# Graph network of four layers: the weighted sum of one layer on VectorE instead of TensorE, and later places for the work behind the sums

## The chip, the cores and the metric

The kernel runs on one core of a Trainium2 chip. The metric is the time of one launch on the device, in microseconds, from the median of several runs; lower is better. The five engines are named as the profile names them: PE is TensorE (its weight loads are listed apart as PEld), DVE is VectorE, ACT is ScalarE, POOL is GpSimd and SP is SyncE.

## The reference, cut to what matters

Four graph layers are applied to `x`, 4096 rows of 256 float32 values. `adj` is a 4096 x 4096 matrix of 0 and 1; it is sparse (each row has itself and a few neighbours, some 9 in the mean), so an attention over all 4096 columns comes down to a weighted sum over each row's neighbours.

```python
h = relu(layernorm(x)); x = x + L0(h, adj)   # four heads, elu of the result
h = relu(layernorm(x)); x = x + L1(h, adj)   # one head
h = relu(layernorm(x)); x = x + L2(h, adj)   # four heads, with a bias
h = relu(layernorm(x)); x = x + L3(h, adj)   # dot products, four heads

# L0, and L2 in the same form
Wh = (h @ W).reshape(n, heads, d)
e = leaky_relu(s_i[:, None, :] + s_j[None, :, :], 0.2)   # s_i, s_j: Wh times two vectors
alpha = softmax(where(adj == 0, -inf, e), axis=1)
out = einsum('ijh,jhd->ihd', alpha, Wh)                  # L0 returns elu(out)

# L1: the neighbours' own rows are summed, not their products
h = node @ W
att = softmax(where(adj > 0, leaky_relu(s1[:, None] + s2[None, :], 0.01), NEG_INF), axis=1)
return h + att @ node

# L3
scores = q @ k.T / 8 + mask;  ctx = softmax(scores) @ v   # for each head, with biases
```

## The kernel before, in words

**The part that the change doesn't touch** takes the first 522 us or so. `scan` and `edges` turn the adjacency matrix into a list of up to 23 neighbours for every row. `first_table` writes the table of layer 0 (a row's product, with its two score terms). `early` takes the first six neighbours of each row in layer 0 already, and `sort` orders the rows by their number of neighbours into 32 blocks of 128 rows. Since the rows of a block have about the same number of neighbours, a block needs a fixed number of gathered rows, `CAPS`: 23 for the first, 3 for the last, 277 in the sum. In layer 0 only what exceeds six is left (93 in the sum, in 23 blocks).

**The layers** are four calls of `layer(l)`. Each walks over the 32 blocks in `ORDER`, a large block and a small one in turn. For one block the steps are:

- `fill(i)` has POOL issue the gathers of the blocks to come, up to `AHEAD` = 4 blocks ahead. Each gather (`fetch`, L529) is one indirect DMA that brings one neighbour for each of the 128 rows. They land in `s_ring`, a ring in SBUF with room for 69 gathered rows in layers 0 and 2, 64 in layer 1 and 36 in layer 3. A gather into a place waits until the last reader of that place is done. In layer 0 each block's own row is gathered as well; in layer 3 it is loaded by SP's queue.
- `scores` (L661 to L697) is DVE work on the block's gathered rows: the score terms are added, leaky_relu, the maximum, the subtraction; ACT then makes the exponentials, `s_p` (L697), in PSUM. In layer 1 it also checks the lists (`mutual`). In layer 3 the scores are products of 256 elements with the query: ACT first copies the query to PSUM (`s_q`), then DVE multiplies (L680) and reduces (L683), eight gathered rows at a time.
- `weigh` (L732 to L753): DVE sums the exponentials, inverts and scales them (L732 to L734); DVE scales the block's own row (L741), and PE adds it to a sum `s_acc` in PSUM by a product with the identity matrix (L745). Then, eight gathered rows at a time, DVE scales them in place (L749) and PE adds each to the sum by one more product with the identity (L753). PE's products with the identity are so 277 + 32 in each of the layers 1, 2 and 3, each of 256 float32 columns.
- `settle` adds the sum to `x`: L777 and L778 in layer 0 (with ACT's part of elu ahead of it), L780 in layers 1 and 2, L772 in layer 3. Then follows the layernorm of the next layer: `norms_of` has DVE's statistics (L382, L383), ACT's Ln and Exp (L386, L388), then four small DVE operations and ACT's relu (L507).
- `turned` has PE transpose the result (L515) and ACT copy it out of PSUM (L516); `times` has PE make the product with the next layer's weights (L522).
- `advance` has DVE take that product out of PSUM (L793 for layer 0's blocks, L800 for layer 1's, L807 and following for layer 2's) and write the next layer's table: POOL scatters it with an indirect DMA (L535) in layer 0, SP's queue sends it in layers 1 and 2 (L801, L808). In layer 3 POOL scatters the finished rows to the output with the same L535.

All layers hold the same loop. The order of the instructions on each engine is the order in which the program writes them (`manual_schedule`); the framework adds only the waits. So the order in the loop sets what each engine does first. With b the i-th block of the order, c the one before it and d the one before that, the loop writes: the gathers of the blocks ahead; the first part of c's settling; b's scores; d's norm, transposes and product; b's weighing; the rest of c's settling; and what comes after d's product. POOL's scatters stand behind that. A layer's first gathers need the whole table of the layer before.

PSUM has eight banks of 512 float32 columns. Before, two hold sums (`s_pacc`), three hold transposes and products (`s_pp`), one holds the query and two the exponentials (`s_pe`).

Of the kernel before, what the change touches and what calls it, by code (L numbers as in the profile page):

```python
# [9 lines left out]
F32 = mybir.dt.float32  # L10
# [4 lines left out]
ALU = mybir.AluOpType  # L15
AX = mybir.AxisListType
PSUM = bass.MemoryType.PSUM
DRAM = bass.MemoryType.DRAM

P = 128  # L20
D = 256
# [44 lines left out]
class Sparse:  # L66
# [246 lines left out]
    def first_table(self, pool, rows, r):  # L313
# [8 lines left out]
        for k in range(4):  # L322
# [5 lines left out]
            ps = self.times(self.turned(pool, h, f"t0_{t}"), self.we0, W, f"t0_{t}")  # L328
# [181 lines left out]
    def turned(self, pool, h, name):  # L510
# [3 lines left out]
        for c in range(KC):  # L514
            nc.tensor.transpose(pt[:, ts(c, P)], h[:, ts(c, P)], self.ident)  # L515
        nc.scalar.copy(ht, pt[:, : KC * P].rearrange("p (c r) -> p c r", c=KC))  # L516
        return ht
# [27 lines left out]
    def layers(self):  # L545
        tc, nc, nt = self.tc, self.nc, self.nt
        with ExitStack() as ctx:
            big = ctx.enter_context(tc.tile_pool(name="s_big", bufs=1))
            self.pool = ctx.enter_context(tc.tile_pool(name="s_main", bufs=2))
            self.pacc = ctx.enter_context(tc.tile_pool(name="s_pacc", bufs=2, space=PSUM))  # L550
            self.pp = ctx.enter_context(tc.tile_pool(name="s_pp", bufs=3, space=PSUM))
            self.pe = ctx.enter_context(tc.tile_pool(name="s_pe", bufs=3, space=PSUM))
# [19 lines left out]
    def layer(self, l):  # L572


# [30 lines left out]
        acc, behind, rows = {}, {}, {}  # L605

        def first(c):
            behind[c] = self.settle(l, c, acc.pop(c), made)
            next(behind[c])

        def second(d):
            if l < 3:
                ht = self.turned(self.pool, next(behind.pop(d)), f"{l + 1}_{d}")
                rows[d] = self.advance(l + 1, d, ht, made)
                next(rows[d])

        def third(d):
            if l < 3:
                next(rows.pop(d), None)
# [3 lines left out]

        for i in range(nt):
            fill(i)
            b, c, d = (ORDER[k] if k >= 0 else None for k in (i, i - 1, i - 2))
            if c is not None:
                first(c)
            g = ring[:, held[b][0] : held[b][1], :]
            p = self.scores(l, b, self.rows[b], g)  # L630
            if d is not None:
                second(d)
            acc[b] = self.weigh(l, b, vs.pop(b) if l == 3 else self.rows[b][:, 0:D], g, p)
            del held[b]
            if c is not None:
                next(behind[c])
            if d is not None:
                third(d)
        c, d = ORDER[-1], ORDER[-2]
        first(c)  # L640
        next(behind[c])
        second(d)
        second(c)
        third(d)
        third(c)

    def scores(self, l, b, mine, g):
# [25 lines left out]
        else:  # L673
            q = self.pe.tile([P, D], F32, name=f"s_q_{b}", tag="q", bufs=1)
# [21 lines left out]
        p = self.pe.tile([P, TOPK, H], F32, name=f"s_p_{l}_{b}", tag="p", bufs=2)  # L696
# [18 lines left out]
    def weigh(self, l, b, me, g, p):  # L715
# [22 lines left out]
        acc = self.pacc.tile([P, IB], F32, tag="acc", name=f"s_acc_{l}_{b}")  # L738
# [650 lines left out]
```

## Time and profile before

| what | value |
| --- | --- |
| time of the runs | 2269.25 us, median of 3 (2267.81 to 2284.88) |
| profiled execution | 2277.38 us |
| its span | 2275.6 us |
| mean granted TensorE clock | 0.75 |
| PE busy | 1175.5 us (52%), 3977 instructions |
| PEld busy | 795.2 us (35%), 3999 |
| DVE busy | 1270.9 us (56%), 3688 |
| ACT busy | 444.1 us (20%), 1320 |
| POOL busy | 1212.4 us (53%), 1354 |
| DMA packets | 128244, 313.24 MB, mean 138 GB/s |

Windows of the profile give the busy time of each engine in a stretch, then the mean granted clock of TensorE as a share of full speed, the DMA engines' busy share and the rate. Groups are listed as "line, engine, operation, out<-in by the program's names, count | busy us, mean ns of one | idle time of the engine just ahead of these instructions, and what ended it". "issue" means that nothing which the profile shows was waited for, and "remote" that the releaser is not among the instructions recorded on this core. Timeline lines have the start in us, the duration in us and the instruction; in brackets the idle time ahead of it on its engine and what ended it. The ends of matmuls are modelled, and a few of their records can be missing.

### The profile page before, as it was taken

The numbers are of one execution on the slowest core, as the hardware profiler recorded it, in microseconds if no ns is written. First come the engines' busy times: TensorE is split into PE (matmuls) and PEld (weight loads), VectorE is DVE, ScalarE is ACT, GpSimd is POOL, SyncE is SP. The second block draws the span as 40 slices with busy tenths as digits, with TensorE's granted clock in tenths as the row PEclk, the third lists the DMA queues.
The fourth block names the chain that finished last, engine by engine and source line by source line (L and its number), as shares of the span: only waits on it lengthen the run. The fifth ranks groups of instructions, "written<-read, shape, count | busy, mean of one in ns | idle before, by whom it ended". The sixth has DMA issues, their size and how long they took to land. (4 is left out here: it accounts for less than half of the span.)

```text
span 2275.6 us, 17106 instructions
## 1 busy us (share of the span) xinstructions
PE 1175.5 (52%) x3977; PEld 795.2 (35%) x3999; DVE 1270.9 (56%) x3688; ACT 444.1 (20%) x1320; POOL 1212.4 (53%) x1354
## 2 busy tenths in 40 slices
PE   4767677611466613454566333566668242445354
PEld 2434334301344402333445222344446131334233
DVE  7657787711466711444466313455569465667666
ACT  5754343000233300111111101112123100000000
POOL 1055666556455457566653375655660465666662
PEclk9887889855687855677788756778789665667777
DMA  8988885305233244333432243333331555666662
GB/s 271 297 288 308 300 259 178 88 13 108 75 99 102 76 88 114 93 104 106 111 104 73 57 110 86 102 100 93 109 107 45 145 171 156 182 181 184 179 180 66
DMA packets 128244, 313.24 MB, mean 138 GB/s; under 512 B 31844, under 2 KB 58983, under 8 KB 128136
## 3 DMA queue, kind: packets, MB, share of 16 engines
q0 software_dynamic: 69088, 207.53, 33.3%
q1 hardware_dynamic: 59048, 104.55, 13.6%
q8 instruction: 34, 0.56, 0.1%
q14 instruction: 74, 0.61, 0.1%
HBM read 276.91 MB, written 35.07 MB: 137 GB/s over the span
## 5 line engine op out<-in xcount | busy, mean ns | idle before, releaser
L529 POOL DMA_INDIRECT s_ring<-s_tab,s_near x924 | 878.0, 950 | 599.5 <-issue 239.8
L753 PE MATMUL s_acc<-s_ring,s_ident 128*128 128x256 f32 x1848 | 510.0, 434 | 80.8 <-issue 59.9
L753 PEld LDWEIGHTS s_acc<-s_ring,s_ident 128*128 128x128 f32 x1848 | 409.6, 224 | 179.1 <-issue 73.6
L745 PE MATMUL s_acc<-s_me,s_ident 128*128 128x256 f32 x256 | 107.7, 511 | 410.6 <-issue 135.3
L749 DVE TENSOR_TENSOR s_ring<-s_ring,s_p 128x256 f32<-128x256 f32 (+7 forms) x169 | 267.1, 1605 | 0.0
L529 POOL DMA_INDIRECT s_g<-s_tab,s_listrow x192 | 184.2, 960 | 113.0 <-issue 53.9
L301 DVE MAX8 s_cand<-s_pt 128x8 f32<-128x256 f32 x512 | 188.4, 419 | 81.6 <-remote 40.5
L745 PEld LDWEIGHTS s_acc<-s_me,s_ident 128*128 128x128 f32 x256 | 61.7, 253 | 436.0 <-issue 232.8
L522 PE MATMUL s_ps<-s_we_l,s_ht 128*128 128x264 f32 x256 | 107.5, 560 | 129.7 <-ACT s_ht L516 92.2
L780 DVE TENSOR_TENSOR s_rx<-s_rx,s_acc 128x256 f32<-128x256 f32 x64 | 26.7, 418 | 246.5 <-remote 240.0
L697 ACT ACTIVATE s_p<-s_e 128x32 f32<-128x32 f32 (+13 forms) x119 | 23.1, 194 | 715.1 <-DVE s_e L693 252.5
L293 PE MATMUL s_pt<-s_low,s_mark 128*128 128x512 fp8e4 x256 | 110.2, 430 | 95.9 <-DVE s_cand L301 45.1
L286 ACT ACTIVATE s_low<-s_raw 128x1024 fp8e4<-128x1024 int32 x128 | 134.5, 1051 | 55.0 <-DMA s_raw<-in_adj_dram 45.1
L522 PE MATMUL s_ps_kv<-s_wkv,s_ht 128*128 128x512 f32 x128 | 88.5, 829 | 94.2 <-issue 69.3
L370 PE MATMUL s_ae<-s_g,s_ident 128*128 128x256 f32 x384 | 111.0, 449 | 19.8 <-issue 11.2
L522 PEld LDWEIGHTS s_ps<-s_we_l,s_ht 128*128 128x128 f32 x256 | 59.9, 259 | 156.2 <-ACT s_ht L516 104.3
L299 PE MATMUL s_pt<-s_places,s_stands 128*128 128x512 bf16 x235 | 100.9, 430 | 0.0
L370 PEld LDWEIGHTS s_ae<-s_g,s_ident 128*128 128x128 f32 x384 | 84.5, 226 | 45.2 <-issue 17.0
L680 DVE TENSOR_TENSOR s_ring<-s_ring,s_q 128x2048 f32<-128x2048 f32 (+7 forms) x48 | 81.0, 1687 | 25.5 <-DMA s_ring<-s_tab,s_near 25.2
L515 PE MATMUL s_pht<-s_ident,s_h 128*128 128x128 f32 x128 | 28.9, 310 | 127.9 <-issue 88.1
L386 ACT ACTIVATE s_y<-s_mv,s_eps 128x1 f32<-128x1 f32 x96 | 28.3, 295 | 312.8 <-DVE s_mv L383 130.9
L772 DVE TENSOR_TENSOR s_out<-s_rx,s_acc 128x256 f32<-128x256 f32 x32 | 13.4, 418 | 133.4 <-remote 99.6
(180 smaller groups left out, 1591.3 us busy)
## 6 DMA issues: line engine op xcount, KB each, us to landing
s_raw<-in_adj_dram SPq DMA_DIRECT2D x128, 512.0 KB
s_ring<-s_tab,s_near POOLq DMA_INDIRECT x924
s_tab<-s_kv SPq DMA_DIRECT2D x32, 256.0 KB
s_own<-s_to SPq DMA_DIRECT2D x32, 134.0 KB
s_tab<-s_rows SPq DMA_DIRECT2D x8, 528.0 KB
s_tab<-s_rx SPq DMA_DIRECT2D x32, 132.0 KB
s_xl<-in_x_dram SPq DMA_DIRECT2D x8, 512.0 KB
s_own<-s_xl SPq DMA_DIRECT2D x8, 512.0 KB
```

What stands on the lines that cost most here:

```text
L286: nc.scalar.activation(lo[:, ts(h, quarter)], raw, AF.Copy, saturate=False, accum_out=sums[:, r, h : h + 1],)
L293: nc.tensor.matmul(pt, lhsT=self.mark, rhs=lo[:, ts(g, IB)], start=True, stop=False)
L299: nc.tensor.matmul(pt, lhsT=stands[:, g, :], rhs=places, start=False, stop=True)
L301: nc.vector.max(out=cand[:, g * (IB // CH) + k, :], in_=pt[:, ts(k, CH)])
L370: nc.tensor.matmul(acc[:, :D], lhsT=self.ident, rhs=g[:, k, 0:D], start=False, stop=(k == E - 1))
L515: nc.tensor.transpose(pt[:, ts(c, P)], h[:, ts(c, P)], self.ident)
L522: self.nc.tensor.matmul(ps[:, :width], lhsT=ht[:, c, :], rhs=w[:, c, :], start=(c == 0), stop=(c == KC - 1),)
L529: self.nc.gpsimd.indirect_dma_start(out=out, out_offset=None, in_=table[:, :], in_offset=bass.IndirectOffsetOnAxis(ap=idx, axis=0),)
L680: nc.vector.tensor_tensor(kq, kq, q.unsqueeze(1).to_broadcast([P, m, D]), ALU.mult)
L745: nc.tensor.matmul(acc[:, :D], lhsT=self.ident, rhs=mev, start=True, stop=(K == 0))
L749: nc.vector.tensor_tensor(v, v, p[:, k0 : k0 + m, :].unsqueeze(3).to_broadcast([P, m, H, D // H]), ALU.mult)
L753: nc.tensor.matmul(acc[:, :D], lhsT=self.ident, rhs=g[:, k0 + k, v0 : v0 + D], start=False, stop=(k0 + k == K - 1),)
```

## The change

1. In layer 1 the weighted sum is made by DVE alone: the own row is scaled into `s_acc` in PSUM, and then each gathered row is multiplied by its weight and added to `s_acc` with one `scalar_tensor_tensor`. DVE's scaling of gathered rows (L749) and own row (L741) and PE's products with the identity (L745, L753) are gone in this layer. Its weights `s_p` lie in SBUF instead of PSUM.
2. `turned` becomes a generator that stops between the transposes and the copy, so that other work can be written between the two.
3. The loop has a new order, with lags `S` and `N` that differ between layers. In layer 1 a block is settled at the end of its own round i (before: at the end of round i + 1); its norm and transposes are written at the start of round i + 1, ahead of the next block's scores (before: after the scores of round i + 2); the copy and the product follow those scores; and what comes after the product is written in round i + 2, right after the scores (before: at the end of round i + 2). In the layers 0, 2 and 3 a block's sum is settled two rounds later (before: one), after that round's scores (before: at the round's end); norm and transposes are three rounds later (before: two), ahead of the scores, with the copy and the product behind them; what comes after the product is four rounds later (before: two), right after the scores. POOL's scatters stand where that last step stands; in layer 3 a finished block is scattered right after the scores of the round that follows its settling (before: at the end of the round of its settling). The end of the layer is written out for the blocks that are left.
4. PSUM is shared out anew: four banks for sums, three for transposes and products as before, and one, `s_shares`, that holds the exponentials of two blocks in turn (in 96 columns each) and the query of layer 3 (in the last 256 columns).
5. The scaled own rows (`s_me`) have three buffers instead of two.

```diff
-        return ht
+        yield None
+        nc.scalar.copy(ht, pt[:, : KC * P].rearrange("p (c r) -> p c r", c=KC))
+        yield ht
...
-            self.pacc = ctx.enter_context(tc.tile_pool(name="s_pacc", bufs=2, space=PSUM))
+            self.pacc = ctx.enter_context(tc.tile_pool(name="s_pacc", bufs=4, space=PSUM))
+            shares = ctx.enter_context(tc.tile_pool(name="s_pe", bufs=1, space=PSUM))
             self.pp = ctx.enter_context(tc.tile_pool(name="s_pp", bufs=3, space=PSUM))
-            self.pe = ctx.enter_context(tc.tile_pool(name="s_pe", bufs=3, space=PSUM))
+            self.turns = 0
+            self.shares = shares.tile([P, IB], F32, name="s_shares")
...
-        def first(c):
-            behind[c] = self.settle(l, c, acc.pop(c), made)
-            next(behind[c])
-        def second(d):
-            if l < 3:
-                ht = self.turned(self.pool, next(behind.pop(d)), f"{l + 1}_{d}")
-                rows[d] = self.advance(l + 1, d, ht, made)
+        def settle(c, parts=(0, 1)):
+            if 0 in parts and c in sums:
+                behind[c] = self.settle(l, c, sums.pop(c), made)
+                next(behind[c])
+            if 1 in parts and c in behind:
+                next(behind[c])
+        def norm(d):
+            if l < 3 and d in behind:
+                turning[d] = self.turned(self.pool, next(behind.pop(d)), f"{l + 1}_{d}")
+                next(turning[d])
+        def product(d):
+            if d in turning:
+                rows[d] = self.advance(l + 1, d, next(turning.pop(d)), made)
                 next(rows[d])
         def third(d):
-            if l < 3:
+            if d in rows:
                 next(rows.pop(d), None)
             for send in made:
                 self.send(*send)
             made.clear()
+        S, N = (0, 1) if l == 1 else (2, 3)
         for i in range(nt):
             fill(i)
-            b, c, d = (ORDER[k] if k >= 0 else None for k in (i, i - 1, i - 2))
-            if c is not None:
-                first(c)
+            b, c, d, e = (ORDER[k] if k >= 0 else None for k in (i, i - S, i - N, i - N - 1))
+            if S:
+                settle(c, (0,))
+            norm(d)
             g = ring[:, held[b][0] : held[b][1], :]
             p = self.scores(l, b, self.rows[b], g)
-            if d is not None:
-                second(d)
-            acc[b] = self.weigh(l, b, vs.pop(b) if l == 3 else self.rows[b][:, 0:D], g, p)
+            third(e)
+            if S:
+                settle(c, (1,))
+            product(d)
+            sums[b] = self.weigh(l, b, vs.pop(b) if l == 3 else self.rows[b][:, 0:D], g, p)
             del held[b]
-            if c is not None:
-                next(behind[c])
-            if d is not None:
-                third(d)
-        c, d = ORDER[-1], ORDER[-2]
-        first(c)
...
+            if not S:
+                settle(b)
+        z, y, x, w = ORDER[-1:-5:-1]
+        if S:
+            settle(y)
+            norm(x)
+            third(w)
+            product(x)
+            settle(z)
+            norm(y)
+            third(x)
+            product(y)
+        norm(z)
+        third(y)
+        product(z)
+        third(z)
...
-            q = self.pe.tile([P, D], F32, name=f"s_q_{b}", tag="q", bufs=1)
+            q = self.shares[:, IB - D :]
...
-        p = self.pe.tile([P, TOPK, H], F32, name=f"s_p_{l}_{b}", tag="p", bufs=2)
+        if l == 1:
+            p = pool.tile([P, TOPK, H], F32, name=f"s_p_{l}_{b}", tag="p", bufs=2)
+        else:
+            p = self.shares[:, ts(self.turns % 2, TOPK * H)].rearrange("p (k h) -> p k h", h=H)
...
-        acc = self.pacc.tile([P, IB], F32, tag="acc", name=f"s_acc_{l}_{b}")
+        acc = self.pacc.tile([P, IB], F32, tag="acc", name=f"s_acc_{l}_{b}")[:, :D]
+        self.turns += 1
+        if l == 1:
+            nc.vector.tensor_scalar(acc, me, p[:, K, :], None, ALU.mult)
+            for k in range(K):
+                nc.vector.scalar_tensor_tensor(
+                    acc, g[:, k, 0:D], p[:, k, :], acc, ALU.mult, ALU.add
+                )
+            return acc
...
-        mev = pool.tile([P, D], F32, name=f"s_me_{l}_{b}", tag="me", bufs=2)
+        mev = pool.tile([P, D], F32, name=f"s_me_{l}_{b}", tag="me", bufs=3)
```

## The prediction

> **What bounds the kernel now.** I read the page's header and groups first, then the windows view with one window per layer, then the groups, waits and timeline of layer 1. The four layers start at about 522, 812, 1282 and 1784 us (first gathers on POOL); what lies before 522 us is untouched. Windows, one per layer, with mean granted clock, DMA share and GB/s at the end:
>
> ```profile
> core 0: us, PE busy (x) PEld busy (x) DVE busy (x) ACT busy (x) POOL busy (x), PEclk, DMA share, GB/s
> 522.00:812.00 290.00, 145.59 (x442) 100.52 (x442) 154.81 (x618) 80.86 (x279) 151.71 (x157) 0.73 0.34 90
> 812.00:1282.00 470.00, 228.45 (x810) 173.25 (x810) 219.80 (x755) 58.13 (x192) 262.71 (x277) 0.73 0.37 97
> 1282.00:1784.00 502.00, 277.44 (x938) 188.49 (x938) 257.33 (x752) 85.80 (x290) 263.13 (x277) 0.77 0.35 92
> 1784.00:2276.00 492.00, 207.50 (x621) 150.87 (x621) 302.13 (x406) 19.66 (x95) 295.10 (x309) 0.68 0.57 165
> ```
>
> No engine is full, yet PE plus POOL comes to 297, 491, 541 and 503 us: within 8% of each layer's length. Three shorter stretches (same columns) tell why:
>
> ```profile
> 866.00:926.00 60.00, 5.96 (x11) 2.77 (x10) 0.54 (x1) 0.00 (x0) 37.72 (x40) 0.53 0.36 97
> ...
> 1234.00:1264.00 30.00, 26.68 (x116) 20.53 (x114) 27.93 (x106) 7.67 (x26) 0.00 (x0) 1.00 0.07 23
> ...
> 1720.00:1762.00 42.00, 37.25 (x148) 26.36 (x146) 39.32 (x121) 13.64 (x46) 0.00 (x0) 1.00 0.09 32
> ```
>
> While POOL gathers, PE and DVE nearly stop; once POOL has nothing left, DVE runs at 93% (7.0 to 7.3 us a block in layer 1, 8.1 to 8.5 in layer 2, by the starts of L697). The timeline inside the first stretch shows the mechanism:
>
> ```profile
> 863.86 0.17 DVE L734 TENSOR_TENSOR s_p<-s_p,s_t 128x4 f32<-128x4 f32 x1 [1.24 <-issue]
> ...
> 865.26 0.42 DVE L741 TENSOR_TENSOR s_me<-s_rx,s_p 128x256 f32<-128x256 f32 x1 [1.23 <-DVE s_p L734]
> ...
> 868.75 0.38 PE L753 MATMUL s_acc<-s_ring,s_ident 128*128 128x256 f32 x1 [2.42 <-issue]
> ...
> 871.55 0.58 PE L753 MATMUL s_acc<-s_ring,s_ident 128*128 128x256 f32 x1 [2.42 <-issue]
> ...
> 874.35 0.58 PE L745 MATMUL s_acc<-s_me,s_ident 128*128 128x256 f32 x1 [2.22 <-issue]
> ```
>
> A matmul and its weight load get through every 2.80 us (1.4 us an instruction) while POOL issues a gather every 1.25; in POOL's pauses the matmuls come 0.22 to 0.43 us apart. Who pays, by the groups of layer 1:
>
> ```profile
> L529 POOL DMA_INDIRECT s_ring<-s_tab,s_near x277 | 262.7, 948 | 158.0 <-issue 93.3 <-remote 27.0 <-ACT s_ht L516 10.6
> L753 PE MATMUL s_acc<-s_ring,s_ident 128*128 128x256 f32 x554 | 144.0, 416 | 19.5 <-issue 19.4
> L749 DVE TENSOR_TENSOR s_ring<-s_ring,s_p 128x2048 f32<-128x2048 f32 (+7 forms) x48 | 79.6, 1686 | 0.0
> ...
> L800 DVE TENSOR_TENSOR s_rx<-s_ps,s_be_l 128x264 f32<-128x264 f32 x32 | 13.7, 427 | 56.9 <-PE s_acc L753 36.1 <-PE s_ps L522 18.5 <-PE s_acc L745 2.4
> ...
> L780 DVE TENSOR_TENSOR s_rx<-s_rx,s_acc 128x256 f32<-128x256 f32 x32 | 13.4, 418 | 128.4 <-remote 125.3 <-PE s_acc L753 2.3 <-issue 0.9
> L516 ACT COPY s_ht<-s_pht 128x256 f32<-128x256 f32 x32 | 11.9, 373 | 127.9 <-remote 110.5 <-PE s_pht L515 14.0 <-PE s_acc L753 3.4
> ```
>
> L780 can wait for nothing but PE's sum and L516 for nothing but PE's transposes, so "remote" is PE finishing late. DVE loses 128.4 + 56.9 = 185 us of 470 to it.
>
> **What the Trainium skill says.** "SBUF — State Buffer", Who interferes with whom: PE and ACT never wait on anyone. The trace disagrees (2.80 us a matmul beside gathers, 0.22 without), and I go by the trace. "TensorE: Matmul & The Clock Gate", specifications: PE's queue is 64 deep, and matmuls keep program order. That agrees: the records ran at 0.22 us until 865.5 and only then fell to one per 2.80, as when a queue has filled. "Perfetto Trace Analysis", Tensor Engine Instruction: a matmul's end is estimated. Agrees: no matmul record stands where L780 was released at 926.98. "PSUM — Partial Sum Buffer", PSUM bank collisions: two engines must be kept apart by bank, not by address; so ACT's and DVE's work in the one bank of `shares` goes one after another. No run here shows it yet.
>
> **The change part by part.**
>
> *Layer 1's weighted sum moves to DVE.* PE loses 554 + 64 matmul records (144.0 + 27.5 = 171 of 228 us) and keeps 2 transposes and 4 product matmuls a block: 12 instructions with their loads, against 51. DVE loses L749 (79.6) and L741 (13.5) and gains 277 chained multiply-adds and 32 scalings. No such instruction with a PSUM output is in the trace; the nearest row is
>
> ```profile
> L778 DVE SCALAR_TENSOR_TENSOR s_rx<-s_acc,s_ex 128x256 f32<-128x256 f32 x32 | 13.6, 424 | 1.1
> ```
>
> and "VectorE: DVE Perf Modes", The TRN2 errata, prices fp32 with two tensors at (256 + 151)/0.96 = 424 ns. A dependent instruction follows 0.03 us later (L780 to L382), so 0.45 each. From below, no gain under 0.27 us (one element a cycle); from above the 1.4 us that L733 to L741 took near 863. I take 0.45. A block of 8.66 gathered rows then costs DVE: scores 1.95 (1063.59 to 1065.54), norm chain 0.75, totals 0.60, own row 0.45, chain 3.90, settling 1.28, L800 0.43, and a new wait of 0.40, since the norm chain now follows its block's Ln and Exp (0.55 us, 0.15 of it under L387) with nothing between. Sum 9.8 us, 315 us in all. POOL needs 277 x 1.25 = 346 us, 10.8 a block, and with 64 ring slots and no send of its own in this layer it need not stop. PE needs 12 x 0.7 = 8.4 us (four instructions took 2.1 to 2.8 us in mid-layer bursts) to 12 x 1.4 = 16.8 us; the upper end would hold DVE at L800. I take 11.1 us a block, little over POOL's: 35 us until the first block has landed (847), 355, and 10 for the drain: 400 against 470, **-70**. From both sides: 373 (POOL alone) to 470.
>
> *Later places in layers 0, 2 and 3.* Settling goes from one block back to two, the norm from two to three, the rest from two to four. DVE now asks after the scores of block i for the sum of i-2 and the product issued one round earlier; before, at the end of round i, for the sum of i-1 and that round's product. PE gets some 0.4 round more, about 3 us. Most of the waits look removable: layer 2 has 115 us at L780, 68.5 of it the first block's, which stays because PE is held until POOL stops, and 55 at L807; layer 3 has 133 us at L772; layer 0 has 52 at L777 (28 stay) and 17 at L793. But PE's own work in these layers is the same and still crawls while POOL gathers; a DVE that waits less lets POOL gather more. I give back most: -20, -25 and -15 us, each between -60 and +10.
>
> *POOL's sends* (layers 0 and 3, one of 1.0 us a block) are behind two more blocks of gathers. POOL now stands 73.5 us for L795 and 46.3 for L772; that is what lets it run ahead, and is in the figures above. Layer 0's first burst grows by two blocks, about 9 gathers or 11 us in which PE is held; in its +10.
>
> *The shared bank.* In layers 0 and 2 Exp must follow the last L749 of the block before, which DVE has already passed before the scores: nothing, by DVE's own order. In layer 3 ACT's copy of q waits for that L749, and L680 for the copy, with nothing of DVE between: 0.36 + 2 x 0.03, so 0.42 x 32 = **+13 us**, less where DVE is not last. I count +10: layer 3 makes -15.
>
> *The rest at nothing.* The third `s_me` and the four sums are buffers; the split of `turned` issues the same copy, behind Exp (0.2 us) on ACT under DVE's weighing; without that cover 0.4 us a block. The drain holds one more block, 3 us a layer; included.
>
> **Sum.** -15 - 70 - 20 - 15 = -120 us from the profiled execution's 2277.4 (span 2275.6): 2157. It stood 8 us above the median of the runs, 2269.25: about 2150.
>
> **The rivals.** (1) *POOL alone bounds all layers.* The waits go wholly: 157 x 1.25 + 55 = 251, 373, 346 + 65 = 411, 309 x 1.25 + 50 = 436 us; minus 283, so 1990. For it: DVE's undisturbed 7 to 9 us a block is under POOL's. Against: layers 0, 2 and 3 keep all PE work. (2) *The wait moves to L800.* With POOL never pausing, PE stays at 1.4 us an instruction; 16.8 us a block fills the ring, POOL stops, PE catches up: 14 us a block, layer 1 at about 460, no gain elsewhere: 2260. For it: PE's pace in every early burst; against: 12 instructions instead of 51. (3) *Slower: DVE's chain in layer 1 takes PE's place in the jam.* Each dependent instruction takes 1.4 us beside POOL, as L733, L734 and L741 near 863: 5.9 + 8.66 x 1.4 = 18 us a block, 576 us, +106: 2375. It decides from 1.0 us a link on (5.9 + 8.66 = 14.6, today's block). Against: L661 to L693 at 847 to 850 ran 0.2 us apart under the same gathers; DVE was slow only beside a full PE queue.
>
> **How the numbers follow.** Forecast 0.60 (2060 to 2225 by the layers' bounds), rival 1 0.12, rival 2 0.16, rival 3 0.12. The range drops rival 3 and the lower part of rival 1: 2020 to 2275; the forecast's own is 2060 to 2225. About 1% (23 us) is what can be told from no change: faster takes the forecast, rival 1 and a third of rival 2, 0.77; the same 0.11; slower rival 3, 0.12.
>
> **What would show it.** Right: layer 1 near 400 us, POOL's gathers near 1.25 us apart, links of 0.45 us on DVE, L780's wait gone there; in the other layers less waiting at the settling lines, with POOL busier and PE slower. Wrong: links near 1 us, a wait of several us a block at L800, or layer 2 or 3 shorter by more than 60 us, which would say that PE's crawl depends on how DVE waits.

## The result, and the profile after

The changed kernel took 2279.32 us (median of 12 runs, 2271.66 to 2287.38) against 2272.59 us for the kernel before on the same chip (12 runs): a ratio of 1.003, 95% interval 1.001 to 1.006. The forecast was 2150 us. The profiled execution took 2280.21 us, its span 2278.2. The line numbers of the kernel after are up to 32 higher: L529 is L531, L749 is L781, L780 is L812, L800 is L832, L807 is L839.

The windows of the kernel after, one for each layer (busy time of each engine, clock, DMA share, GB/s):

```profile
525.00:806.00 281.00, 142.05 (x442) 103.04 (x442) 152.80 (x617) 77.79 (x279) 151.04 (x158) 0.70 0.34 93
806.00:1305.00 499.00, 90.08 (x192) 46.76 (x192) 287.02 (x984) 53.45 (x192) 262.40 (x277) 0.50 0.34 91
1305.00:1808.00 503.00, 268.80 (x941) 188.25 (x941) 257.69 (x752) 82.93 (x290) 263.62 (x278) 0.77 0.34 92
1808.00:2278.00 470.00, 212.93 (x619) 153.29 (x618) 302.66 (x406) 22.09 (x94) 294.83 (x309) 0.68 0.58 172
```

Layer 0 went from 291 to 281 us, layer 1 from 469 to 499, layer 2 from 502 to 503, layer 3 from 491 to 470. PE's work in layer 1 fell from 228 to 90 us (the forecast's sum leaves 57; at a granted clock of 0.50 instead of 0.73 a product took 0.69 us, L524, instead of 0.56), and the layer got longer. The groups of layer 1 (busy and mean of one, then the idle time ahead of them and its releasers):

```profile
L531 POOL DMA_INDIRECT s_ring<-s_tab,s_near x277 | 262.8, 949 | 168.1 <-issue 130.3 <-DVE s_acc L767 16.0 <-DMA s_tab<-s_rx,s_near 2.3
L767 DVE SCALAR_TENSOR_TENSOR s_acc<-s_ring,s_p,s_acc 128x256 f32<-128x256 f32 x277 | 135.7, 490 | 22.1 <-DVE s_acc L767 12.7 <-DVE s_acc L765 0.2
...
L832 DVE TENSOR_TENSOR s_rx<-s_ps,s_be_l 128x264 f32<-128x264 f32 x32 | 13.6, 425 | 3.7 <-PE s_ps L524 3.7
L812 DVE TENSOR_TENSOR s_rx<-s_rx,s_acc 128x256 f32<-128x256 f32 x32 | 13.5, 421 | 2.8 <-DVE s_acc L767 1.8
```

The waits at the settling line and at the product (L780 and L800 before, 185 us) are gone: 2.8 and 3.7 us. Yet DVE is idle for 190 us of the layer in gaps over 0.1 us. Of these 38 are the first gather and 13 the wait for Exp; 3.7 stand at L832, and some 135 us are left. The timeline of DVE in the layer's first run of gathers shows what they are:

```profile
845.98 3.12 DVE L767 SCALAR_TENSOR_TENSOR s_acc<-s_ring,s_p,s_acc 128x256 f32<-128x256 f32 x6
849.95 0.49 DVE L767 SCALAR_TENSOR_TENSOR s_acc<-s_ring,s_p,s_acc 128x256 f32<-128x256 f32 x1 [0.86 <-DVE s_acc L767]
851.36 0.49 DVE L767 SCALAR_TENSOR_TENSOR s_acc<-s_ring,s_p,s_acc 128x256 f32<-128x256 f32 x1 [0.92 <-DVE s_acc L767]
852.75 0.49 DVE L767 SCALAR_TENSOR_TENSOR s_acc<-s_ring,s_p,s_acc 128x256 f32<-128x256 f32 x1 [0.90 <-DVE s_acc L767]
...
866.75 0.42 DVE L812 TENSOR_TENSOR s_rx<-s_rx,s_acc 128x256 f32<-128x256 f32 x1 [0.90 <-DVE s_acc L767]
```

Six links (a link is one multiply-add of the chained sum) took 3.12 us, 0.525 each with the gap. From 849 us on a link passes every 1.40 us, with nothing to wait for but DVE's own link before it, while PE has no instruction at all between 839 and 866 us. It is the pace that PE had before (1.40 us an instruction), now on DVE. I call this a hold-up. In mid-layer it comes at the end of each of POOL's runs of gathers (lines of DVE, then POOL's next gather):

```profile
1003.98 0.16 DVE L394 SCALAR_TENSOR_TENSOR s_rn<-s_y 128x1 f32<-128x1 f32 x1 [1.23 <-DVE s_y L392]
...
1009.58 0.44 DVE L733 TENSOR_REDUCE s_has<-s_eq 128x12 f32<-128x276 bf16 x1 [4.08 <-remote]
1010.29 0.17 DVE L734 SCALAR_TENSOR_TENSOR s_has<-s_away,s_has 128x12 f32<-128x12 f32 x1 [0.27 <-DVE s_has L733]
1010.99 0.17 DVE L737 TENSOR_REDUCE s_both<-s_has 128x1 f32<-128x12 f32 x1 [0.53 <-DVE s_has L734]
```

```profile
1014.29 0.95 POOL L531 DMA_INDIRECT s_ring<-s_tab,s_near  x1 [6.13 <-issue]
```

L733 reads only what L729 wrote, which had ended at 1005.49; so what came late can only be DVE's own completion, and "remote" says no more than that its releaser is not recorded. POOL's run had begun at 987 us; DVE was undisturbed for its first 15 us (some 12 gathers) and held until about 3 us after its last gather (1007.2). Then POOL itself stood for 6.13 us, since its next slots in the ring were freed only by the links from 1013 us on. So two blocks took some 27 us instead of the 20 that DVE needs: at the end of the layer, when POOL has little left to fetch, the blocks took 9.9 to 10.6 us each.

### The profile page after: what moved, and what is told of

The parts are those of the page before. It is cut to its first block, busy times and chain, and to the rows that moved or that the text cites. A ratio compares the mean times of both kernels' runs of the same rounds, so it can differ in the third digit from the quotient of the medians.

```text
span 2278.2 us, 16059 instructions
## 1 busy us (share of the span) xinstructions
PE 1040.2 (46%) x3381; PEld 677.8 (30%) x3381; DVE 1337.2 (59%) x3917; ACT 435.9 (19%) x1320; POOL 1212.1 (53%) x1354
## 4 chain that ended last, share of the span: by engine, by line
DVE 37%; issue 19%; PE 15%; another core or an unknown queue 13%; POOL 7%; DMA 6%; ACT 3%; DVEq 0%; SPq 0%; ACTq 0%; POOLq 0%
DVE s_acc L767 7%; DVE s_ring L781 4%; PE s_acc L785 4%; PE s_ae L371 3%; POOL s_ring L531 3%; PE s_ps_kv L524 3%; POOL s_g L531 2%; DVE s_cand L301 2%; DVE s_ring L701 2%; DVE s_e L704 2%; DVE s_st L383 1%; DMA s_ring<-s_tab,s_near 1%; DMA s_raw<-in_adj_dram 1%; POOL s_lists L446 1%
## 5 line engine op out<-in xcount | busy, mean ns | idle before, releaser
L531 POOL DMA_INDIRECT s_ring<-s_tab,s_near x924 | 877.7, 950 | 641.2 <-issue 277.6
L785 PE MATMUL s_acc<-s_ring,s_ident 128*128 128x256 f32 x1294 | 379.1, 453 | 66.0 <-issue 48.1
L785 PEld LDWEIGHTS s_acc<-s_ring,s_ident 128*128 128x128 f32 x1294 | 297.9, 233 | 145.7 <-issue 65.5
L777 PE MATMUL s_acc<-s_me,s_ident 128*128 128x256 f32 x192 | 79.2, 502 | 406.8 <-issue 176.9
L531 POOL DMA_INDIRECT s_g<-s_tab,s_listrow x192 | 184.2, 959 | 114.7 <-issue 53.2
L524 PE MATMUL s_ps<-s_we_l,s_ht 128*128 128x264 f32 x256 | 118.6, 609 | 159.7 <-ACT s_ht L518 103.1
L781 DVE TENSOR_TENSOR s_ring<-s_ring,s_shares 128x2048 f32<-128x2048 f32 (+7 forms) x121 | 187.4, 1572 | 0.0
L777 PEld LDWEIGHTS s_acc<-s_me,s_ident 128*128 128x128 f32 x192 | 42.3, 239 | 429.0 <-issue 189.8
L767 DVE SCALAR_TENSOR_TENSOR s_acc<-s_ring,s_p,s_acc 128x256 f32<-128x256 f32 x277 | 135.7, 490 | 22.1 <-DVE s_acc L767 12.7
L524 PE MATMUL s_ps_kv<-s_wkv,s_ht 128*128 128x512 f32 x128 | 86.0, 808 | 133.1 <-ACT s_ht L518 73.9
L524 PEld LDWEIGHTS s_ps<-s_we_l,s_ht 128*128 128x128 f32 x256 | 65.8, 284 | 192.0 <-ACT s_ht L518 117.5
L516 PEld LDWEIGHTS s_pht<-s_ident,s_h 128*128 128x128 f32 x128 | 18.2, 172 | 340.0 <-issue 226.0
L701 DVE TENSOR_TENSOR s_ring<-s_ring,s_shares 128x2048 f32<-128x2048 f32 (+7 forms) x48 | 81.1, 1690 | 53.2 <-DMA s_ring<-s_tab,s_near 34.0
L299 PE MATMUL s_pt<-s_places,s_stands 128*128 128x512 bf16 x256 | 111.5, 436 | 0.0
L721 ACT ACTIVATE s_shares<-s_e 128x32 f32<-128x32 f32 (+8 forms) x87 | 17.3, 198 | 388.9 <-DVE s_e L714 144.5
```

Source lines behind the costliest of these rows:

```text
L299: nc.tensor.matmul(pt, lhsT=stands[:, g, :], rhs=places, start=False, stop=True)
L524: self.nc.tensor.matmul(ps[:, :width], lhsT=ht[:, c, :], rhs=w[:, c, :], start=(c == 0), stop=(c == KC - 1),)
L531: self.nc.gpsimd.indirect_dma_start(out=out, out_offset=None, in_=table[:, :], in_offset=bass.IndirectOffsetOnAxis(ap=idx, axis=0),)
L701: nc.vector.tensor_tensor(kq, kq, q.unsqueeze(1).to_broadcast([P, m, D]), ALU.mult)
L767: nc.vector.scalar_tensor_tensor(acc, g[:, k, 0:D], p[:, k, :], acc, ALU.mult, ALU.add)
L777: nc.tensor.matmul(acc, lhsT=self.ident, rhs=mev, start=True, stop=(K == 0))
```

## The experiments

Layer lengths (us) come from each profile, by POOL's first gather of a layer; ratios are to the kernel before, timed on the same chip in the same session.

| run | layer 0 | layer 1 | layer 2 | layer 3 | median us | ratio, 95% interval |
| --- | --- | --- | --- | --- | --- | --- |
| before | 291 | 469 | 502 | 491 | 2272.59 | |
| after | 281 | 499 | 503 | 470 | 2279.32 | 1.003 (1.001 to 1.006) |
| e1_sum_only | 288 | 494 | 506 | 476 | 2286.30 | 1.007 (1.004 to 1.009) |
| e2_lags_only | 280 | 478 | 507 | 472 | 2252.37 | 0.991 (0.987 to 0.995) |
| e3_pace250 | 283 | 463 | 513 | 472 | 2240.38 | 0.985 (0.981 to 0.990) |
| e4_pace500 | 278 | 469 | 501 | 470 | 2246.23 | 0.989 (0.986 to 0.993) |
| e5_pace_all250 | 264 | 463 | 481 | 472 | 2197.45 | 0.968 (0.964 to 0.971) |
| e6_two_chains | 281 | 483 | 507 | 467 | 2255.58 | 0.994 (0.991 to 0.997) |
| e7_lumps | 278 | 452 | 493 | 472 | 2223.52 | 0.981 (0.977 to 0.985) |
| e9_lumps2 | 285 | 481 | 507 | 472 | 2252.74 | 0.988 (0.981 to 0.994) |
| e10_pe_lumps2 | 283 | 458 | 514 | 469 | 2237.23 | 0.978 (0.970 to 0.987) |
| e11_all_lumps2 | 261 | 481 | 504 | 472 | 2232.02 | 0.979 (0.973 to 0.985) |
| e12_before_lumps2 | 272 | 452 | 482 | 482 | 2217.87 | 0.975 (0.968 to 0.982) |

A layer that two kernels have in common differs by up to some 20 us from run to run (layer 2: 493 to 514 us over the runs that leave it as it is after the change), so single layers are read with that in mind.

**Which part costs.** The first run is the kernel before with the sum on DVE alone, the second the kernel after with the sum back on PE.

```diff
+        if l == 1:
+            nc.vector.tensor_scalar(acc[:, :D], me, p[:, K, :], None, ALU.mult)
+            for k in range(K):
+                nc.vector.scalar_tensor_tensor(
+                    acc[:, :D], g[:, k, 0:D], p[:, k, :], acc[:, :D], ALU.mult, ALU.add
+                )
+            return acc[:, :D]
```

> The kernel before with one part of the change: layer 1's weighted sum on VectorE, with the old order of the loop and the old PSUM shares. Theory (POOL's long run of gathers delays each completion on every other engine, so the chained sum on VectorE is held up as TensorE's products were): layer 1 takes about 500 us (470 before), with links 1.4 us apart in the layer's first run of gathers; the whole is about 2305 us. Rival (the sum on VectorE is a gain, and the new order of layer 1 spoils it): layer 1 takes about 400 us and the whole about 2200 us.

```diff
-        S, N = (0, 1) if l == 1 else (2, 3)
+        S, N = 2, 3
...
-            for k in range(K):
-                nc.vector.scalar_tensor_tensor(
-                    acc, g[:, k, 0:D], p[:, k, :], acc, ALU.mult, ALU.add
-                )
```

> The changed kernel with layer 1's sum back on TensorE and with the lags of the other layers in layer 1 too. Theory: layers 0, 2 and 3 stay at 281, 503 and 470 us, layer 1 goes from 500 back to about 465 us (its length before, less the few us that the later places gave elsewhere); the whole is about 2243 us. Rival (the later places or the shared bank cost layer 1 its time, not the sum on VectorE): layer 1 stays at about 500 us and the whole at 2278 us.

Under the old order layer 1 took 494 us with the sum on DVE and 469 with it on PE; under the new lags 499 and 478. So the sum on DVE costs 21 to 25 us here, little over what single layers differ by, but the whole times agree: the sum alone loses 0.7%, the later places alone gain 0.9%, both clear of their intervals. The rivals fell in both.

**Is it POOL's run of gathers?** POOL is given more to do: a memset on one partition behind each gather of layer 1.

```diff
                     self.fetch(ring[:, s + k, :], self.tab[l], at_k)
+                    nc.gpsimd.memset(self.idle[:, :250], 0.0)
```

> The changed kernel with a POOL memset of 250 elements on one partition behind each gather of layer 1: POOL has more to do, some 0.3 us a gather, 277 x 0.3 = 83 us in all. Theory (VectorE sets the pace of layer 1 and is held up when POOL gathers without a pause for over 15 us): with gathers 1.55 us apart the hold-ups shrink, and layer 1 falls from 500 to about 445 us (277 x 1.55 = 429, and the drain), the whole to about 2225 us. Rival (POOL and the ring's space set the pace, VectorE's gaps are only waiting): layer 1 gets longer by up to 83 us, the whole is 2280 to 2360 us.

> As the run before, with 500 elements: about 0.55 us more a gather, so that gathers are 1.8 us apart. Theory: no hold-ups are left, but POOL itself now bounds layer 1: 277 x 1.8 = 499 us and the drain of some 20, so about 515 us, the whole about 2295 us, with links of 0.52 us on VectorE everywhere. Rival (POOL and the ring set the pace): 150 us more in layer 1, the whole about 2430 us.

With 82 us more work on POOL layer 1 fell from 499 to 463 us; with 140 us more it took 469. In the second, all 245 distances of two links are 0.525 us, as expected; the layer is 277 x 1.61 + 23 us, POOL's own time (a memset takes the place of part of the 0.30 us between gathers, so that gathers were 1.61 us apart and not 1.8: my price of the memset was too high). At 1.41 us between gathers 30 links were still held, most of them to 0.70 us apart. So the distances seen are 1.40 us a link at 1.25 us a gather, mostly 0.70 at 1.41, none held at 1.61. The rival, a ring or POOL that sets the pace, is out: more work on POOL made the layer shorter.

The same pause in lumps, five memsets of 470 elements after every 8 gathers:

> The changed kernel with the same time given to POOL in layer 1 as in the first paced run, but in lumps: after every 8 gathers five memsets of 470 elements, about 2.4 us. Theory as it stands (hold-ups begin after about 12 gathers in a row and end some 4 us after POOL stops): a pause of 2.4 us in every 12.4 us is enough or nearly so, layer 1 takes about 455 us, the whole about 2235 us. Rival (only the distance of two gathers counts): inside a run of 8 the gathers are 1.25 us apart as before, and the hold-ups stay: layer 1 500 us or more, the whole 2280 us or more.

452 us, and again no held link. The groups of its layer 1 have DVE waiting almost only for gathers (13 us besides for Ln and Exp):

```profile
L689 DVE TENSOR_TENSOR s_e<-s_ring,s_rx 128x9 f32<-128x9 f32 (+12 forms) x32 | 5.5, 173 | 122.6 <-DMA s_ring<-s_tab,s_near 122.3
```

122 us of waiting for data and POOL's 346 + 82 us of work: POOL is the bound, and a pause of 2.4 us in every 12.4 us is enough. Two memsets instead of five (1.0 us) are not:

> The changed kernel with two memsets of 470 elements (about 1.0 us) after every 8 gathers of layer 1, in place of the five that made POOL the bound (452 us, no held link). POOL then has 277 x 1.25 + 34 x 1.0 = 380 us. If so short a pause is enough (theory, in its strong form): layer 1 takes about 405 us, the whole about 2175 us. If the hold-ups need the 4 us that the traces show from POOL's stop to the release (rival): layer 1 takes 450 to 490 us, the whole 2230 to 2270 us.

481 us, with 25 links held: the expectation of 405 us failed, the rival's range holds.

**What is it that is counted?** The gathers of layer 1 are cut to 128 bytes a row; the weighted sum then adds what lies in the ring, the ring is cleared ahead of the layer, and the neighbours are not renumbered.

```diff
-                    self.fetch(ring[:, s + k, :], self.tab[l], at_k)
+                    slim = self.tab[l].rearrange("n (a w) -> (n a) w", w=WL - D)
+                    self.fetch(ring[:, s + k, D:], slim, at_k)
...
-                nc.scalar.copy(self.near[:, b, 0:K], g[:, :, WL - 1])
```

> The changed kernel with gathers of 128 bytes a row instead of 1152 in layer 1: the first 256 elements of each row are left out of the gather (what lies in the ring is summed in their place, and the ring is cleared ahead of the layer), and the renumbering of the neighbours is left out. Theory A (the number of gathers that POOL issues counts): hold-ups as before, layer 1 about 500 us. Theory B (the bytes or the DMA engines' load count): no hold-ups, links of 0.52 us throughout, layer 1 about 38 + 32 x 10 = 360 us.

Only layer 1 of this run, of one execution, is read (behind the sparse way it went through the kernel's second, dense one, and its total of 10792 us has both). Its window, and its timeline at the same place:

```profile
810.00:1296.00 486.00, 90.12 (x192) 46.80 (x192) 286.73 (x984) 50.27 (x160) 261.57 (x278) 0.50 0.09 19
```

```profile
858.24 0.49 DVE L772 SCALAR_TENSOR_TENSOR s_acc<-s_ring,s_p,s_acc 128x256 f32<-128x256 f32 x1 [0.91 <-DVE s_acc L772]
858.89 0.94 POOL L531 DMA_INDIRECT s_ring<-s_tab,s_near  x1 [0.30 <-issue]
859.64 0.49 DVE L772 SCALAR_TENSOR_TENSOR s_acc<-s_ring,s_p,s_acc 128x256 f32<-128x256 f32 x1 [0.91 <-DVE s_acc L772]
```

19 GB/s instead of 91, DMA engines at 0.09 instead of 0.34, and the same 1.40 us a link. So it is not the bytes. Whether it is POOL's issuing, or something that comes with every gather whatever it carries (its 128 rows, its landing), this run doesn't tell apart.

**Latency or rate?** Every other link goes into a second sum, so that a link doesn't need the one just before it.

```diff
+            nc.vector.tensor_scalar(two, g[:, 0, 0:D], p[:, 0, :], None, ALU.mult)
+            for k in range(1, K):
+                to = acc if k % 2 else two
+                nc.vector.scalar_tensor_tensor(
+                    to, g[:, k, 0:D], p[:, k, :], to, ALU.mult, ALU.add
+                )
+            nc.vector.tensor_tensor(acc, acc, two, ALU.add)
```

> The changed kernel with layer 1's sum as two chains, every other row into a second sum in SBUF, and one addition more a block (32 x 0.45 = 14 us), so that a link does not depend on the link just before it. Theory (in a long run of gathers one instruction of an engine is completed every 1.4 us, dependent or not): links of the first run stay 1.4 us apart, layer 1 takes about 510 us, the whole 2290 us. Rival (a dependent instruction waits 1.4 us for the one before it): two links pass in 1.4 us, layer 1 takes about 480 us, the whole 2260 us.

The links of the first run stayed 1.40 us apart, so it is a rate of completions and not a longer latency of each. The layer still took 483 us and not 510: undisturbed links were 0.39 us apart instead of 0.525, some 245 x 0.13 = 32 us less against 14 for the additions, which I had not counted.

**PE under the same pauses, and the other layers.**

> The changed kernel with the 250-element memset behind each gather of all four layers. Theory (POOL's unbroken run of gathers holds up every other engine, TensorE above all): layers 0, 2 and 3 gain as layer 1 did. Layer 2 falls from 503 to about 460 us, layer 0 from 281 to about 265; layer 3, whose POOL has 309 x 1.25 = 386 us of work already, stays near 470, since 309 x 1.55 = 479. Layer 1 463 as in the paced run of layer 1 alone. The whole is about 2180 us. Rival (only VectorE's chained sum is held up, TensorE waits for something else): layers 0, 2 and 3 get longer by 10 to 40 us each, the whole is about 2290 us.

> The same pauses in layer 1 with the sum on TensorE there (the kernel with the lags alone, 478 us in layer 1). This compares the two places of the sum under equal pauses. Theory (an instruction is held up whatever its engine, and the sum on TensorE has 51 instructions a block with their loads against some 31 on VectorE): TensorE gains too, but less: about 440 us against 405. Rival (VectorE's sum is at its own limit of 10 us a block, TensorE's is not): TensorE is as fast or faster, 405 us or less.

> The changed kernel with the two memsets after every 8 gathers in all four layers. Theory: layer 0 about 265 us, layer 1 as in the run with layer 1 alone, layer 2 about 460 us (503 without), layer 3 about 455 us (470); with 405 us in layer 1 the whole is about 2105 us. Rival (layers 2 and 3 are held by TensorE's own work, not by hold-ups): they get no shorter, the whole is about 2180 us.

> The kernel before with the same pauses in all four layers: it has the sum on TensorE everywhere and the old lags. Theory: every layer gains, since TensorE's crawl was the same hold-up: layer 1 from 469 to about 435 us, layer 2 from 502 to about 470, layer 3 from 491 to about 475, layer 0 from 291 to about 280; the whole about 2180 us. Rival (the pauses help only VectorE's chain): no layer gains, and POOL's additional 115 us make it 2270 to 2330 us.

With the memset of 250 behind every gather layer 0 fell by 17 us and layer 2 by 22, layer 3 not at all: 0.968, the best under hold-ups. The kernel before gained by the short pauses too, 0.975, 9 to 20 us in each layer, so PE's crawl too goes with POOL's long runs. Under the short pauses in layer 1 the sum on PE was faster (458 us) than on DVE (481): neither number was expected, and the order of the two was the rival's, though the intervals of the two ratios overlap. The short pauses in all layers of the kernel after brought layer 0 to 261 us, but did nothing for layers 2 and 3 (504 and 472), against the expectation. Why the same pauses shortened layer 2 of the kernel before (482) and not of the kernel after is not shown.

**Two sessions without hold-ups.** Four runs were to tell the two places of the sum apart under longer pauses:

> The kernel with the lags alone (layer 1's sum on TensorE), with three memsets of 470 elements (about 1.4 us) after every 8 gathers of layer 1. With two it took 458 us there. If the pause is the lever: 440 to 450 us, the whole about 2225 us. If TensorE's own work is what is left: no shorter than 458 us.

> The changed kernel (layer 1's sum on VectorE) with the same three memsets. With two it took 481 us in layer 1, with five 452 us, there bound by POOL. POOL's own time is now 277 x 1.25 + 34 x 1.44 = 395 us. If VectorE's chain is as good as TensorE's products once the hold-ups are short: within 5 us of the other run. If the sum on VectorE is worse in itself (10 us a block of VectorE work against 7): 15 to 25 us longer, about 465 us, the whole about 2240 us.

> The kernel with the lags alone and four memsets (about 1.9 us) after every 8 gathers of the layers 0, 1 and 2, none in layer 3, where POOL is near its bound. Theory (hold-ups are what these layers lose): layer 0 about 262 us, layer 1 about 440, layer 2 about 475, layer 3 472: the whole about 2170 us, the best of the study. Rival (the pauses of one layer only): layer 2 stays above 495 us, the whole about 2200 us.

> The changed kernel with the same four memsets in layers 0, 1 and 2. It differs from the run before in layer 1's sum alone. If the two places of the sum are equal once hold-ups are short, the two kernels agree within 5 us (both about 2170 us); if the sum on VectorE is worse in itself, this one is 10 to 25 us slower.

They met other conditions: the kernel before took 1944 us there. The pauses now cost what POOL needs for them. Ratios were 1.010 (1.007 to 1.012), 1.010 (1.007 to 1.013), 1.069 (1.066 to 1.072) and 1.065 (1.062 to 1.068); layer 1 took 421 us with the sum on PE and 415 on DVE under three memsets, 442 and 437 under four, in each case POOL's time and some 20 to 30 us. How the two places compare under hold-ups they did not answer; without them the whole times are within 7 us. Both kernels as they are were run once more:

> The changed kernel as it is, for a second trace, beside a trace of the kernel before on the same chip. In the last four runs the chip was another one, on which the kernel before took 1944 us and no hold-up stood in the traces. If this chip is of that kind: POOL bounds every layer, layer 0 about 222 us, layer 1 about 277 x 1.25 + 20 = 366, layer 2 about 377, layer 3 about 427, the whole about 1910 us and about 0.98 of the kernel before. If it is of the kind of the others: about 2280 us, 1.00 of the kernel before, with links 1.40 us apart in the first run of gathers.

> The kernel before as it is, on the same chip. If this chip shows no hold-ups: TensorE's matmuls beside gathers come 0.2 to 0.5 us apart, nothing waits for them, and the layers are 10 to 15 us longer than the changed kernel's by the settling close behind the sums: about 1944 us. If it shows them: 2270 us, with a matmul and its load in 2.80 us in the first run of gathers.

The conditions were the same as in the four runs: 1914.11 us (1909.77 to 1916.08) for the kernel after, 1939.91 for the kernel before, a ratio of 0.987 (0.984 to 0.989). Windows of the kernel before by layer:

```profile
509.00:754.00 245.00, 133.55 (x442) 93.99 (x442) 154.69 (x617) 80.68 (x279) 151.72 (x158) 0.80 0.39 106
754.00:1123.00 369.00, 222.19 (x810) 171.31 (x810) 221.74 (x755) 59.02 (x192) 261.61 (x277) 0.80 0.46 123
1123.00:1497.00 374.00, 261.93 (x941) 182.09 (x941) 258.30 (x752) 86.51 (x290) 263.17 (x277) 0.87 0.46 124
1497.00:1927.00 430.00, 198.72 (x619) 145.86 (x618) 302.80 (x406) 19.54 (x94) 294.22 (x309) 0.71 0.63 188
```

and of the kernel after:

```profile
510.00:731.00 221.00, 126.85 (x442) 93.95 (x442) 153.54 (x618) 77.73 (x279) 151.50 (x157) 0.79 0.43 118
731.00:1102.00 371.00, 90.15 (x192) 46.87 (x192) 287.25 (x984) 53.45 (x192) 262.45 (x278) 0.50 0.46 122
1102.00:1480.00 378.00, 260.79 (x939) 186.31 (x940) 255.40 (x752) 84.16 (x290) 262.57 (x278) 0.86 0.45 123
1480.00:1908.00 428.00, 220.82 (x621) 159.11 (x620) 302.77 (x406) 22.09 (x94) 293.93 (x309) 0.71 0.63 189
```

Busy times over the span are within 4% of the first traces' (PE's in layer 0 is 8 to 11% less); the time between is gone: 336 us in the sum of the layers before (1418 against 1754), 355 after (1398 against 1753). Links run on beside gathers (the timeline of DVE after, 19 links in one line, 0.525 us each), and so do matmuls (of PE before, 46 records):

```profile
770.63 9.94 DVE L767 SCALAR_TENSOR_TENSOR s_acc<-s_ring,s_p,s_acc 128x256 f32<-128x256 f32 x19
```

```profile
793.30 11.72 PE L753 MATMUL s_acc<-s_ring,s_ident 128*128 128x256 f32 x46 [0.98 <-DVE s_ring L749]
```

Each layer is now near POOL's own time: 277 x 1.25 = 346 us and 23 to 32 in layers 1 and 2. The sum on DVE is worth nothing there (371 us against 369). The whole gain is layer 0, 245 to 221 us. The groups of POOL's sends in layer 0 say why, first before, then after:

```profile
L535 POOL DMA_INDIRECT s_tab<-s_rx,s_near x32 | 31.9, 998 | 52.0 <-ACT s_rx L795 37.3 <-ACT s_ex L767 9.0 <-issue 3.4
```

```profile
L537 POOL DMA_INDIRECT s_tab<-s_rx,s_near x32 | 31.8, 995 | 29.1 <-ACT s_rx L827 5.3 <-issue 5.3 <-ACT s_ht L518 4.5
```

POOL waits 23 us less for rows to send, since they are asked for two rounds later. Under hold-ups most of the same wait stayed (98.0 us before, 89.9 after).

## Why the prediction was wrong, point by point

**Layer 1, forecast -70, measured +30: the step that failed.** The price was set by "A dependent instruction follows 0.03 us later (L780 to L382), so 0.45 each", and the third rival was put aside with "DVE was slow only beside a full PE queue". The kernel after has DVE at 1.40 us a link with PE idle, so PE's queue isn't needed for it: in a long run of POOL's gathers the instructions of DVE and PE, whichever is working, are held (e3, e4, e7: shown by taking the long runs away). Moving the sum from PE to DVE moved the hold-up with it. The third rival's mechanism was right at its place, its size was not: 1.4 us held for 14 links and at the end of each later run, not for all 277; the mean distance, (231 x 0.525 + 14 x 1.40) / 245 = 0.575 us, stayed under the 1.0 us from which it decides. Nor does the trace contradict the Trainium skill's sentence that PE and ACT never wait on anyone, as the prediction has it: its section is about engines that share SBUF ports, and no run here shows that a port is what holds PE.

**The terms of the sum.** An undisturbed link took 0.525 us and not 0.45 (busy 0.49 where the price taken was 0.424), 23 us over 277 links and 32 scalings; the block's 9.8 us was nearly right all the same, 9.9 to 10.6 at the end of the layer. That POOL, "with 64 ring slots and no send of its own in this layer", need not stop was wrong under hold-ups: it stood 5 to 9 us in almost every run of a pair of blocks, 86 us in all, for slots that DVE's held work had yet to free (without hold-ups it stopped once, for 2.3 us). PE's share was overrated: L832 waited 3.7 us.

**Layer 2, forecast -20, measured +1.** The wait at the settling line fell and came back at the product, as two lines of the kernel before and two of the kernel after show:

```profile
L780 DVE TENSOR_TENSOR s_rx<-s_rx,s_acc 128x256 f32<-128x256 f32 x32 | 13.4, 418 | 118.1 <-remote 114.7 <-PE s_acc L753 3.3
L807 DVE TENSOR_TENSOR s_kv<-s_ps_kv,s_bqkv 128x512 f32<-128x512 f32 x32 | 22.1, 692 | 57.0 <-PE s_ps_kv L522 55.5 <-issue 1.4
```

```profile
L839 DVE TENSOR_TENSOR s_kv<-s_ps_kv,s_bqkv 128x512 f32<-128x512 f32 x32 | 22.0, 687 | 106.4 <-PE s_ps_kv L524 106.3
L812 DVE TENSOR_TENSOR s_rx<-s_rx,s_acc 128x256 f32<-128x256 f32 x32 | 13.1, 411 | 60.8 <-remote 60.6 <-PE s_acc L785 0.2
```

175 us became 167. That a later place doesn't help where PE is held for longer than the place is moved is my reading; no run varies the lag here.

**Layers 0 and 3, forecast -15 each, measured -10 and -21.** Right in sign; the size is in part luck, since these layers in e1, where they are as before, took 288 and 476 us (-7 and -6), and without hold-ups the change gave -24 and -2. The cost of the shared bank, forecast 0.42 x 32 = 13 us at L680, stands in the trace without hold-ups: DVE's multiply by the query waits 14.7 us for ACT's copy (L696), where the kernel before waited for no copy. This agrees with "PSUM — Partial Sum Buffer", PSUM bank collisions, in the Trainium skill, which asks that semaphores keep two engines apart by bank; the wait can also come from the program's own order of reads and writes in that tile, which no run here tells apart. It was covered: layer 3 took 428 us against 430.

**The first rival, POOL alone,** gave 251, 373, 411 and 436 us for the layers. Without hold-ups they took 221, 371, 378 and 428. Where hold-ups are absent it was near in the whole (1990 us forecast, 1914 measured), with layers 0 and 2 some 30 us too long, and the forecast's own -70 was wrong there too, since the kernel before is at POOL's bound already.

**Open.** What makes a hold-up is not shown. It came after some 12 gathers in a row, and with pauses of only 1.0 us behind every 8 (e9), doesn't depend on their bytes, and lets one instruction pass per 0.70 or 1.40 us. It was in the traces of all sessions in which the kernel before took 2270 to 2277 us and in none of the last two (1944 and 1940 us), while a gather took 0.95 us and followed after 0.30 in both. A lasting property of one chip isn't it, if the number on record names the same chip each time: chip 4 had hold-ups in e9 to e12 (2277 us) and none in the last two runs (1940 us).

The traces themselves differ in one thing: their records of DMA landings. A page tells a group's time from issue to landing only where the number of landing records fits that of the issues. The kernel before with hold-ups, then without:

```profile
s_ring<-s_tab,s_near POOLq DMA_INDIRECT x924
s_ring<-s_tab,s_near POOLq DMA_INDIRECT x924, 3.0
```

Without hold-ups the trace of the kernel after has 4944 landing records for the 308 DMAs of layer 1, 16 each; with them it has 1373 for 309, 4.4 each. In e4 and e7, where no link of layer 1 was held, it is 15.6 and 9.2 each there, in e3 and e9, where some were, 5.5 and 4.8. In the held stretch shown above, from 849 to 866 us, 24 semaphore events are recorded, 12 of DVE and 12 landings, one per 0.69 us: half the distance of the held links. So hold-ups stand where the recording falls behind. Recording is the rival that no run here tests: it may cause them, or both may follow from something else. Each run on record lists a span and a granted clock, as a trace gives them, so there is none to compare that is known to have been timed without.

That the change leaves the time as it is holds under hold-ups; without them it gains 1.3%. Which of the two a launch without recording would show is open.

## What to carry to other kernels

When an engine looks slow, see whether it is that engine or whoever is working at the time: look for a stretch in which another engine has the same pace, before moving its work there. Where a run of one engine's instructions delays all others, breaking up the run can shorten the whole though it adds work (2.4 us of pause in every 12.4 us, 499 to 452 us in the layer); but such a remedy costs its own time where the delay is absent (1.065), so time both kernels in more than one session, and see first whether the trace is complete: here missing landing records went with the delay. A wait at one line that is relieved by a later place often stands at the next line that needs the same engine.

## What the runs showed of the hardware that was not expected

- In the traces with incomplete landing records, and in unbroken runs of indirect DMAs on POOL (one per 1.25 us), dependent DVE instructions passed one per 1.40 us, and PE's one per 1.40 us; at 1.41 us a gather mostly one per 0.70 us; at 1.61 us undisturbed. With a ninth of the bytes a row (128 against 1152) it was the same.
- The same program took 2270 us in some sessions and 1940 in others, with the same busy time of every engine within 5% over the span; layer 1 had 16 landing records a DMA in the fast ones and about 4 in the others.
- A chained scalar_tensor_tensor of 128x256 float32 into PSUM took 0.49 us and followed its forerunner after 0.525; with two chains in turn, the second into SBUF, 0.39 us apart.
